# Six projections of the last two batches as seven block products each, in an RWKV block on one Trainium2 core

## The chip, the cores and the metric

The kernel runs on one NeuronCore of a Trainium2 chip. It uses TensorE for matrix products (PE in the profile, its weight loads PEld), VectorE (DVE), ScalarE (ACT) and GpSimd (POOL) for elementwise work, and SyncE (SP) to issue DMAs. TensorE writes to PSUM; GpSimd works in SBUF only. The metric is the device time of one execution in microseconds; lower is better.

## The reference

One RWKV block over 8 batches of 256 tokens with 512 channels (32 heads of 16). All in float32. Cut to what matters here:

```python
xn = _ln(x, ln1_w, ln1_b); sx = _token_shift(xn, state[:, i1])
x5 = xn[:, :, None] + sx[:, :, None] * (maa_stack + xxx)     # five mixes
r, k, v = x5[..3] @ Wr.T, x5[..0] @ Wk.T, x5[..2] @ Wv.T     # 512 x 512 each
g = silu(x5[..4] @ Wg.T)
# recurrent scan over the tokens, then a norm over each head: att
x = x + att * g @ Wo.T                                       # "o"
xn2 = _ln(x, ln2_w, ln2_b); sx2 = _token_shift(xn2, state[:, i0])
xk, xr = xn2 + sx2 * ffn_maa_k, xn2 + sx2 * ffn_maa_r
rr = sigmoid(xr @ ffn_Wr.T)                                  # "fr"
kk = square(relu(xk @ ffn_Wk.T))                             # "fk"
x = x + rr * (kk @ ffn_Wv.T)                                 # "fv"
```

So each batch has eight projections by a 512 x 512 matrix, of which the last four (o, fk, fr, fv) come after the scan.

## The kernel before

The kernel collects all its work as a list of some 2,700 operations (`Plan`), each with its engine, the buffers that it reads and writes, and a function that emits it. `Plan.ORDER` is one long list of numbers written out by hand: the operations are emitted in this order, so each engine's queue takes its operations in the order of the list, and a buffer of a pool is given to an operation when the list reaches it.

For each batch there are three stages. `inputs_of_scan` normalizes x, builds the five mixes and makes r, k, v, w and g. `scan` does the recurrence: for each of 16 slices a DMA spreads v over a `vs` tile (128 x 1024), VectorE multiplies it by k (L864; k was copied into PSUM, `kp`, by ScalarE at L845), VectorE scans along the tokens (L866, the decay lies in PSUM as `wrep`), GpSimd multiplies by r (L869, in place in an `st8` tile), and TensorE gathers four such slices (L877). `rest` norms att, multiplies by g (L941 in the last batch), and does the four projections: o with x added (L949), the second layer norm (L493 to L562), fk with relu and square (L958, L959), fr with tanh (L967; the sigmoid is (tanh + 1)/2), and fv, whose result is multiplied by (o + 1) (L990) and gets x added (L995 on GpSimd, or L985 and L993 on VectorE in the last batch) before it is written out.

A projection is 16 matmuls of 128 x 128 by 256 columns, or 8 with 512 columns. `project` (fk) puts channels on the partitions; `project_tokens` (o, fr, fv) puts tokens there, with the two 128-token halves of the activations as the weights of TensorE and rows of the matrix as the moving operand. Both go through `mul` (L330); each matmul in float32 leaves two records in the trace. Results lie in one of six PSUM buffers `ps`.

Weights of the four projections of `rest` are loaded anew for each batch into four `Ws` tiles (128 x 2 x 512, two for each matrix). Other pools that the change uses: `mix` (14 tiles of 128 x 512), `vs` and `st8` (six of 128 x 1024 each), and `k`, `r`, `v`, `w` (three of each, 128 x 512).

The order at the end is this. Projections of batch 6 and 7 are written fr6, fv6, o7, fk7, fr7, fv7. After the last scan and the last gather of batch 7 TensorE does fr6, o7, one half of fv6, the transposes of the layer norm, the other half of fv6, then fk7, fr7 and fv7. fv7's second half of tokens is cut into pieces of 256, 128 and 128 channels, each written out by itself.

Of the kernel before, what the change touches and what calls it, by code (L numbers as in the profile page):

```python
# [11 lines left out]
P = 128  # L12
# [9 lines left out]
AHEAD = (4, 5, 6, 7)  # L22
HALF = 0.5
# [37 lines left out]

class Op:


    def __init__(self, engine, us, outs, ins, emit, mode):
        self.engine, self.us, self.emit, self.mode, self.narrow, self.table = engine, us, emit, mode, False, None
        self.bufs = list(dict.fromkeys([*outs, *ins]))
        self.before, self.wire = [], 0


class Plan:
# [197 lines left out]
def tile_rwkv_block(  # L269
# [44 lines left out]
    def new(pool, name):  # L314
        return Buf(pool, name, VIEWS.get(pool, lambda t: t))
# [780 lines left out]
```

## Time and profile before

| | |
|---|---|
| median of 3 runs | 603.5 us (602.17 to 604.19) |
| the profiled execution | 603.54 us |
| its span, first to last instruction | 601.7 us |
| TensorE busy / VectorE busy / ScalarE busy / GpSimd busy | 592.1 / 537.5 / 504.9 / 507.2 us |
| granted TensorE clock | 0.996 |
| DMA | 128.07 MB, 213 GB/s |

Busy time is the time in which an engine had at least one instruction under way. In a row of the timeline stand start and duration in microseconds, engine, line, operation, output <- inputs by buffer name, shapes, and count; several equal instructions in a row are merged. A group row ends with busy time and the mean duration in nanoseconds. In the rows by stretches of time (from:to) stand the length, the busy time of PE, PEld, DVE, ACT and POOL with the number of instructions, the granted TensorE clock, the DMA share and GB/s.

### The profile page before, as it was taken

The page shows a single profiled execution, that of the slowest core. Times are in us where ns is not written, and L with a number is a line of the kernel's source. Part 1 is how long each engine was busy: PE and PEld are TensorE (multiplying, and loading weights), DVE is VectorE, ACT ScalarE, POOL GpSimd, SP SyncE. Part 2 cuts the span into 40 slices and gives each one's busy share as a digit, 9 for nine tenths or more (in the row PEclk, how much of TensorE's full clock was granted, in tenths as well). Part 3 has the DMA queues.
Part 4 walks back from the last instruction along what each step waited for, and adds up shares of the span by engine and source line. Part 5 has one row for each costly group of instructions (what it writes and reads, how often), then busy time and mean ns, then how long its engine had stood idle before and what let it go on. Part 6 is the DMA issues. An engine that isn't in the chain of part 4 may idle for free.

```text
span 601.7 us, 19771 instructions
## 1 busy us (share of the span) xinstructions
PE 592.1 (98%) x8308; PEld 343.5 (57%) x8308; DVE 537.5 (89%) x500; ACT 504.9 (84%) x1198; POOL 507.2 (84%) x390
## 2 busy tenths in 40 slices
PE   8999998999999999999999999999999999999997
PEld 7575556457536775366553754465645574455464
DVE  5799999999999999899889999999999999996342
ACT  5898779899999999989999988989987879964531
POOL 0689999899989999999979898999798999888030
PEclk9999999899999999999999999999999999999999
DMA  8797768887888869778888897687899887952533
GB/s 295 228 246 196 186 155 246 239 221 203 224 229 246 221 163 276 220 203 230 203 250 221 224 251 212 163 234 206 219 257 242 214 234 206 280 180 73 189 122 109
DMA packets 55497, 128.07 MB, mean 213 GB/s; under 512 B 6112, under 2 KB 13680, under 8 KB 55408
## 3 DMA queue, kind: packets, MB, share of 16 engines
q1 hardware_dynamic: 51040, 122.61, 74.9%
q10 hardware_dynamic: 4368, 4.20, 2.2%
q8 instruction: 65, 1.06, 0.8%
q14 instruction: 24, 0.20, 0.1%
HBM read 118.39 MB, written 8.40 MB: 211 GB/s over the span
## 4 chain that ended last, share of the span: by engine, by line
PE 83%; POOL 10%; ACT 2%; DVE 2%; issue 2%; DMA 0%; SPq 0%; POOLq 0%; ACTq 0%
PE ps L330 70%; PE ps L877 8%; POOL st L869 5%; POOL mix L701 3%; PE ps L741 2%; PE ps L525 2%; POOL vs L861 1%; DVE st L493 1%; POOL rk L814 1%; PE ps L903 1%; DMA sq<-in_x 0%; POOL mix L569 0%; PE ps L819 0%; POOL att L833 0%; POOL mix L729 0%
## 5 line engine op out<-in xcount | busy, mean ns | idle before, releaser
L866 DVE TENSOR_TENSOR_SCAN st<-wrep,vs 128x1024 f32<-128x1024 f32 x128 | 288.2, 2277 | 2.2 <-POOL mix L701 0.6
L869 POOL TENSOR_TENSOR st<-st,r 128x1024 f32<-128x1024 f32 x128 | 254.7, 2002 | 8.3 <-DVE st L866 5.1
L864 DVE TENSOR_TENSOR vs<-vs,ps 128x1024 f32<-128x1024 f32 x125 | 147.7, 1208 | 6.1 <-ACT vs L857 4.1
L330 PE MATMUL ps<-Ws,mix 128*32 128x512 f32 (+3 forms) x836 | 115.5, 585 | 0.0
L330 PEld LDWEIGHTS ps<-Ws,mix 128*32 128x32 f32 (+1 forms) x836 | 39.0, 118 | 61.9 <-issue 54.6
L701 POOL TENSOR_TENSOR mix<-mix,xn 128x512 f32<-128x512 f32 x62 | 67.1, 1095 | 7.1 <-DVE mix L695 4.1
L330 PE MATMUL ps<-mix,Wv 128*32 128x256 f32 (+1 forms) x880 | 62.2, 389 | 2.1 <-POOL mix L701 2.1
L877 PE MATMUL ps<-st,con 128*32 128x256 f32 x1024 | 61.9, 380 | 0.0
L330 PE MATMUL ps<-mix,Wr 128*32 128x256 f32 (+1 forms) x760 | 60.7, 380 | 0.2 <-ACT v L772 0.2
L330 PE MATMUL ps<-mix,Wg 128*32 128x256 f32 (+1 forms) x904 | 60.4, 379 | 0.0
L330 PE MATMUL ps<-mix,Wk 128*32 128x256 f32 (+1 forms) x856 | 59.5, 380 | 0.0
L330 PE MATMUL ps<-mix,Ws 128*32 128x256 f32 (+1 forms) x928 | 57.5, 379 | 0.0
L330 PE MATMUL ps<-Ws,g 128*32 128x512 f32 (+1 forms) x464 | 56.9, 592 | 0.5 <-POOL g L943 0.5
L569 POOL TENSOR_TENSOR mix<-mix,xn 128x512 f32<-128x512 f32 x44 | 47.5, 1091 | 7.3 <-ACT mix L567 7.3
L330 PEld LDWEIGHTS ps<-mix,Wv 128*32 128x32 f32 (+1 forms) x880 | 39.8, 117 | 22.0 <-issue 4.4
L330 PEld LDWEIGHTS ps<-mix,Wr 128*32 128x32 f32 (+1 forms) x760 | 39.5, 119 | 17.2 <-issue 1.1
L827 ACT COPY att<-ps 32x256 f32<-32x256 f32 x128 | 46.5, 364 | 2.7 <-PE ps L819 0.5
L330 PEld LDWEIGHTS ps<-mix,Wg 128*32 128x32 f32 (+1 forms) x904 | 37.2, 114 | 18.9 <-issue 1.0
L330 PEld LDWEIGHTS ps<-mix,Wk 128*32 128x32 f32 (+1 forms) x856 | 38.5, 115 | 16.6 <-issue 1.2
L877 PEld LDWEIGHTS ps<-st,con 128*32 128x32 f32 x1024 | 34.4, 110 | 23.6 <-issue 2.8
L330 PEld LDWEIGHTS ps<-mix,Ws 128*32 128x32 f32 (+1 forms) x928 | 35.9, 113 | 20.3 <-issue 1.2
L689 ACT ACTIVATE ps<-ps,vec 128x256 f32<-128x256 f32 x112 | 44.3, 449 | 3.5 <-PE ps L330 3.1
(134 smaller groups left out, 940.0 us busy)
## 6 DMA issues: line engine op xcount, KB each, us to landing
vs<-vo SPq DMA_DIRECT2D x128, 512.0 KB, 5.9
Ws<-in_fk SPq DMA_DIRECT2D x16, 512.0 KB, 6.2
Ws<-in_fr SPq DMA_DIRECT2D x16, 512.0 KB, 5.2
Ws<-in_wo SPq DMA_DIRECT2D x16, 512.0 KB, 5.9
Ws<-in_fv SPq DMA_DIRECT2D x16, 512.0 KB, 4.9
x<-in_x SPq DMA_DIRECT2D x11, 512.0 KB, 6.3
vo<-v ACTq DMA_DIRECT2D x15, 256.0 KB, 3.7
out<-o SPq DMA_DIRECT2D x15, 256.0 KB, 5.3
```

The source lines that it names most:

```text
L330: nc.tensor.matmul(out[i : i + n], lhsT=w[:, i : i + n], rhs=x, start=first, stop=final)
L493: dve(512, [st], [s], lambda st=st, s=s: nc.vector.bn_stats(out=st(), in_=s()))
L525: nc.tensor.transpose(ps()[:, m, n * P : (n + 1) * P], xh[n]()[:, k * P : (k + 1) * P], idt())
L569: gp(512, t, [t, xn[q]], lambda q=q, t=t: nc.gpsimd.tensor_tensor(t(), t(), xn[q]()[:, :, 1 : T + 1], ALU.add))
L689: act(256, p_, [p_, vec], lambda g=g, q=q, m=m, p_=p_: nc.scalar.activation(p_()[:, m, :], p_()[:, m, :], AF.Identity, bias=col(f"maa_{g}" ...
L701: gp(512, t, [t, xn[q]], lambda q=q, t=t: nc.gpsimd.tensor_tensor(t(), t(), xn[q]()[:, :, 1 : T + 1], ALU.add))
L741: nc.tensor.matmul(pd()[i : i + 32, 0, :], lhsT=w, rhs=src[k // 2]()[:, k % 2, :], start=(k == begin), stop=(k == end))
L827: act(350, atts[q], [pc], lambda i=32 * (2 * q + m), m=m, q=q, h=32 * h: nc.scalar.copy(atts[q]()[h : h + 32, m, :], pc()[i : i + 32, 0, :]))
L864: dve(4 * T, [vs], [vs, kp], lambda m=m, vs=vs, kp=kp: nc.vector.tensor_tensor(vs(), vs(), kp()[:, m : m + 1, :].to_broadcast([P, 4, T]), ...
L866: dve(4 * T, [st], [w, vs], lambda w=w, vs=vs, st=st: nc.vector.tensor_tensor_scan(st().rearrange("p n t -> p (n t)"), w().rearrange("p n ...
L869: gp(4 * T, st, [st, r], lambda m=m, st=st, r=r: nc.gpsimd.tensor_tensor(st(), st(), r()[:, m : m + 1, :].to_broadcast([P, 4, T]), ALU.mul ...
L877: nc.tensor.matmul(pat()[32 * i : 32 * i + 32, 0, :], lhsT=con()[:, s : s + 32], rhs=done[i]()[:, j, :], start=(j == 0), stop=(j == 3),)
```

## The change

Six projections, o7, fk7, fr7, fv7, fr6 and fv6, are done by Strassen's algorithm in Winograd's form. The activations and the matrix are each cut into 2 x 2 blocks; eight block products become seven, and sums of blocks are added around them: four sums of activation blocks (named x0 to x3 below, each 128 x 256 elements), four sums of weight blocks (w0 to w3, 128 x 512), and seven sums of products (128 x 256) for the result. Two lines say which pool holds the weight sums and which engine makes them, and which weights are streamed into `vs` tiles in place of `Ws`:

```diff
+SEVEN = {"o7": ("vs", "DVE"), "fk7": ("st8", "POOL"), "fr7": ("st8", "POOL"), "fv7": ("st8", "POOL"), "fr6": ("krvw", "DVE"), "fv6": ("krvw", "POOL")}
+STREAMS = {"fr7": "vs", "fv7": "vs"}
```

Activation sums are made on VectorE. The core of the new functions:

```diff
+    def tensor(engine, n, out, a, b, how):
+        if engine == "DVE":
+            dve(n, [out], [a, b], lambda: nc.vector.tensor_tensor(out(), a(), b(), how))
+        else:
+            gp(n, out, [a, b], lambda: nc.gpsimd.tensor_tensor(out(), a(), b(), how))
+
+    def seven(name, w, src, tokens=True):
...
+        for out, x, y, how in ((0, a[1, 0], a[1, 1], ALU.add), (1, s[0], a[0, 0], ALU.subtract),
+                               (2, a[0, 0], a[1, 0], ALU.subtract), (3, a[0, 1], s[1], ALU.subtract)):
+            tensor(es, ns, s[out], x, y, how)
+        for out, x, y, how in ((0, b[0, 1], b[0, 0], ALU.subtract), (1, b[1, 1], t[0], ALU.subtract),
+                               (2, b[1, 1], b[0, 1], ALU.subtract), (3, t[1], b[1, 0], ALU.subtract)):
+            tensor(et, nt, t[out], x, y, how)
+        pairs = {1: (a[0, 0], b[0, 0]), 2: (a[0, 1], b[1, 0]), 3: (s[3], b[1, 1]), 4: (a[1, 1], t[3]),
+                 5: (s[0], t[0]), 6: (s[1], t[1]), 7: (s[2], t[2])}
...
+                            mul(out()[:, cols], l()[:, k, :], r()[:, k, cols], k == 0, k == 1)
...
+        one = product(1)
+        act(256, old, [one], lambda: nc.scalar.copy(old(), one()))
+        tensor("DVE", T, spare[0], product(6), old, ALU.add)
+        tensor("DVE", T, spare[1], product(5), spare[0], ALU.add)
+        return product, old, *spare
+
+    def into(blocks, product, old, six, five):
...
+        tensor("DVE", T, blocks[1, 0], six, product(4), ALU.subtract)
+        tensor("DVE", T, blocks[0, 1], five, product(3), ALU.add)
+        last = product(7)
+        tensor("DVE", T, blocks[1, 0], blocks[1, 0], last, ALU.add)
+        tensor("DVE", T, blocks[1, 1], five, last, ALU.add)
+        if (0, 0) in blocks:
+            tensor("DVE", T, blocks[0, 0], old, product(2), ALU.add)
+
+    def added(blocks, product, old, six, five):
...
+        for i, t in (((1, 0), six), ((0, 1), five), ((1, 1), five), ((0, 0), old)):
+            tensor("DVE", T, blocks[i], blocks[i], t, ALU.add)
```

A product is read from PSUM by the sums that use it; `old`, `six` and `five` lie in SBUF, in `mix` tiles. o7 adds its sums straight onto x (`added`); the others write them to kk, o or a spare tile (`into`). relu, square and tanh of these projections, and the closing (o + 1) * y and + x, go by blocks of 256. In the last batch fv7's second product is cut in two halves of 128 channels, and its blocks are written out as each is done.

The list of numbers is new as a whole, from its first line on; the list has 2,811 operations now. At the end it puts the work like this:

- TensorE, from the last gather: fr6's products 1 and 2, the head norm of batch 7, half of g7's first projection (it stood before the last gather), fr6's 6, 3, 5; o7's 1, 2, 5, 6, 3, 4, 7; fv6's 7 and 1, fr6's 4, fv6's 6 and 2, transposes, fv6's 4, transposes, fr6's 7, fv6's 5 and 3; fk7's 2, 3, 1, 5, 6, 4, 7; then fr7 and fv7 mixed, with fr7's 7, fv7's 7, fr7's 3, a half of fv7's 2 and fv7's 3 at the end.
- VectorE, from the last scan: fr6's w0, w1, one (o+1)*y of batch 5, fv6's x2, fr6's w3, w2, the two last att adds, the other (o+1)*y; x0 of fv6, x0 of fr6, x1 of fv6, x1 of fr6, x3 of fv6; o7's w0, fr6's x3, o7's w2, w1; att by its norm twice; o7's w3, the first g product, fr6's x2, the second g product, o7's x0; then the sums of o7 between its x1, x2, x3 and some of fr6.
- GpSimd, from the last scan: the last product by r, xr6 twice, + x of batch 5 twice, weight sums fr7.w0, fv7.w0, fr7.w1, fv7.w1, fv6.w0, w2, w1, w3, fr7.w2, w3, fk7.w0, w2, w1, w3, then sx, fv7.w3, xr7 twice, + x of batch 6 four times, fv7.w2.
- The weight loads of fr6, o7, fr7 and fv7 are issued around the last scan; the second half of fv6's weights follows fr6's third product, fk7's follow o7's.

More of the change, by code (lines that the diff above doesn't have):

```diff
@@ L59, in __call__, with __init__ @@
         return self.view(self.buf())
+class Half(Part):
+    def __init__(self, buf, view):
+        super().__init__(buf, view)
+        self.writers, self.readers, self.before = [*buf.writers], [], set()
+class Group:
+    def __init__(self, parts, view):
+        self.parts, self.view = parts, view
+    def __call__(self):
+        return self.view()
 class Op:
@@ L66, in __init__ @@
         self.engine, self.us, self.emit, self.mode, self.narrow, self.table = engine, us, emit, mode, False, None
-        self.bufs = list(dict.fromkeys([*outs, *ins]))
+        self.bufs = list(dict.fromkeys(getattr(b, "buf", b) for b in [*outs, *ins]))
         self.before, self.wire = [], 0
@@ L206, in add @@
     def add(self, engine, us, outs, ins, emit, mode=None, kb=0, part=False):
-        outs, ins = ([getattr(b, "buf", b) for b in bs] for bs in (outs, ins))
+        outs, ins = ([p if hasattr(p, "writers") else p.buf for b in bs for p in getattr(b, "parts", [b])] for bs in (outs, ins))
         op = Op(engine, us, outs, ins, emit, mode)
@@ L427, in stream @@
     def stream(name, src, b):
-        tiles = [new("Ws", f"W{name}{b}_{h}") for h in range(2)]
+        pool = STREAMS.get(f"{name}{b}", "Ws")
+        tiles = [new(pool, f"W{name}{b}_{h}") for h in range(2)]
+        if pool != "Ws":
+            for t in tiles:
+                t.view = lambda t: t.rearrange("p j t -> p (j t)").rearrange("p (k e) -> p k e", k=2)
         load_pairs(tiles, src)
@@ L597, in project_tokens, with halves @@
         return ps
+    def halves(pool, name, n, width):
+        each = {"mix": 2 * T, "st8": 4 * T, "vs": 4 * T}[pool] // (2 * width)
+        tiles = [new(pool, f"{name}{i}") for i in range(-(-n // each))]
+        return [Half(tiles[i // each], lambda t, j=i % each * 2 * width: t.rearrange("p m t -> p (m t)")[:, j : j + 2 * width]
+                     .rearrange("p (k w) -> p k w", k=2)) for i in range(n)]
+    def tensor(engine, n, out, a, b, how):
[3 more added lines that the diff above has]
+            gp(n, out, [a, b], lambda: nc.gpsimd.tensor_tensor(out(), a(), b(), how))
@@ new lines, in seven, with product, mm @@
+    def seven(name, w, src, tokens=True):
+        pool, engine = SEVEN[name]
+        tile_of = lambda k: k.buf
+        W2, X2 = [tile_of(w[0]), tile_of(w[2])], src
+        wide = {(h, c): Part(W2[h], lambda t, c=c: t[:, :, c * T : (c + 1) * T]) for h in range(2) for c in range(2)}
+        slim = {(h, n): x if isinstance(x, Half) else Part(x, lambda t, n=n: t[:, :, n * P : (n + 1) * P])
+                for h in range(2) for n in range(2) for x in [X2[h][n] if isinstance(X2[h], list) else X2[h]]}
+        ws = (halves(pool, f"tw{name}_", 4, T) if pool != "krvw" else [
+            Part(new(p, f"tw{name}_{p}"), lambda t, lo=int(p == "v"): t[:, :, lo : lo + T]) for p in pool])
+        xs = halves("mix", f"tx{name}_", 4, P)
+        old, *spare = halves("mix", f"old{name}_", 6 if name[:2] == "fv" else 3, P)
+        if tokens:
+            old, *spare = (Half(h.buf, lambda t, h=h: h.view(t).rearrange("p k w -> p (k w)")) for h in (old, *spare))
+        if tokens:
+            a = {i: slim[i[1], i[0]] for i in ((0, 0), (0, 1), (1, 0), (1, 1))}
+            b, s, t, es, et, ns, nt = wide, xs, ws, "DVE", engine, T, 2 * T
+        else:
+            a = {(c, h): wide[h, c] for h in range(2) for c in range(2)}
+            b, s, t, es, et, ns, nt = slim, ws, xs, engine, "DVE", 2 * T, T
+        for out, x, y, how in ((0, a[1, 0], a[1, 1], ALU.add), (1, s[0], a[0, 0], ALU.subtract),
[6 more added lines that the diff above has]
+                 5: (s[0], t[0]), 6: (s[1], t[1]), 7: (s[2], t[2])}
+        def product(i, cols=slice(0, T)):
+            l, r = pairs[i]
+            buf = new("ps", f"pw{name}_{i}")
+            out = Part(buf, lambda t: t[:, 0, :] if tokens else t[:, :, 0:P])
+            def mm():
+                for m in range(1 if tokens else 2):
+                    for k in range(2):
+                        if tokens:
+                            mul(out()[:, cols], l()[:, k, :], r()[:, k, cols], k == 0, k == 1)
+                        else:
+                            mul(out()[:, m, :], l()[:, k, m * P : (m + 1) * P], r()[:, k, :], k == 0, k == 1)
+            pe((0.86 if tokens else 0.89) * (cols.stop - cols.start) / T, [buf], [l, r], mm)
+            return out
+        one = product(1)
[3 more added lines that the diff above has]
+        return product, old, *spare
@@ new lines, in into @@
+    def into(blocks, product, old, six, five):
[9 more added lines that the diff above has]
+            tensor("DVE", T, blocks[i], blocks[i], t, ALU.add)
+        tensor("DVE", T, blocks[1, 0], blocks[1, 0], product(4), ALU.subtract)
+        tensor("DVE", T, blocks[0, 1], blocks[0, 1], product(3), ALU.add)
+        last = product(7)
+        for n in range(2):
+            tensor("DVE", T, blocks[1, n], blocks[1, n], last, ALU.add)
+        tensor("DVE", T, blocks[0, 0], blocks[0, 0], product(2), ALU.add)
@@ L946, in rest @@
         x2 = load_x(b, "x2")
-        for n in range(NT):
-            t, ps = x2[n], project_tokens(Wo, ys, n, f"pso{b}_{n}")
-            dve(512, [t], [ps, t], lambda t=t, ps=ps: nc.vector.tensor_tensor(
-                t(), ps().rearrange("p m t -> p (m t)"), t(), ALU.add))
+        blocks = {(n, c): Half(x2[n].buf, lambda t, n=n, c=c: t[:, n, c * T : (c + 1) * T]) for n in range(NT) for c in range(2)}
+        if f"o{b}" in SEVEN:
+            added(blocks, *seven(f"o{b}", Wo, ys))
+            x2 = [Group([blocks[n, c] for c in range(2)], t) for n, t in enumerate(x2)]
+        else:
+            for n in range(NT):
+                t, ps = x2[n], project_tokens(Wo, ys, n, f"pso{b}_{n}")
+                dve(512, [t], [ps, t], lambda t=t, ps=ps: nc.vector.tensor_tensor(
+                    t(), ps().rearrange("p m t -> p (m t)"), t(), ALU.add))
+            blocks = {(n, c): Part(x2[n].buf, h.view) for (n, c), h in blocks.items()}
         xn, sx = normed(x2, 2, 0, b, last)
@@ L954, in rest @@
         kk = []
-        for q in range(NQ):
+        if f"fk{b}" in SEVEN:
+            ts = [new("mix", f"kk{b}_{q}") for q in range(NQ)]
+            kk = [[Half(t, lambda t, n=n: t[:, :, n * P : (n + 1) * P]) for n in range(NT)] for t in ts]
+            parts = {(q, n): kk[q][n] for q in range(NQ) for n in range(NT)}
+            into(parts, *seven(f"fk{b}", Wfk, xk, False))
+            for t in parts.values():
+                act(256, t, [t], lambda t=t: nc.scalar.activation(t(), t(), AF.Relu, scale=HALF**0.5))
+                act(256, t, [t], lambda t=t: nc.scalar.activation(t(), t(), AF.Square))
+        for q in range(NQ if not kk else 0):
             t = new("mix", f"kk{b}_{q}")
@@ L962, in rest @@
         Wfr = stream("fr", fr, b)
-        os = []
-        for n in range(NT):
+        os, outs = [], {}
+        if f"fr{b}" in SEVEN:
+            os = [new("o", f"o{b}_{n}") for n in range(NT)]
+            outs = {(n, c): Half(os[n], lambda t, c=c: t[:, c * T : (c + 1) * T]) for n in range(NT) for c in range(2)}
+            into(outs, *seven(f"fr{b}", Wfr, xr))
+            for t in outs.values():
+                act(256, t, [t], lambda t=t: nc.scalar.activation(t(), t(), AF.Tanh, scale=HALF), "tanh")
+        for n in range(NT if not os else 0):
             o = new("o", f"o{b}_{n}")
@@ L970, in rest @@
         Wfv = stream("fv", fv, b)
+        if f"fv{b}" in SEVEN:
+            product, old, six, five, *spare = seven(f"fv{b}", Wfv, kk)
+            sums = dict(zip(((0, 1), (1, 0), (1, 1)), spare))
+            if last:
+                into(sums, product, old, six, five)
+                y, x_ = outs[0, 0], blocks[0, 0]
+                dve(T, [old], [y, old], lambda: nc.vector.scalar_tensor_tensor(old(), y(), 1.0, old(), ALU.add, ALU.mult))
+                tensor("DVE", T, x_, x_, old, ALU.add)
+                two = [product(2, slice(h * P, (h + 1) * P)) for h in range(2)]
+            else:
+                sums[0, 0] = old
+                into(sums, product, old, six, five)
+            for i, t in sums.items():
+                o, t2 = outs[i], blocks[i]
+                dve(T, [o], [o, t], lambda o=o, t=t: nc.vector.scalar_tensor_tensor(o(), o(), 1.0, t(), ALU.add, ALU.mult))
+                tensor("DVE" if last else "POOL", T, o, o, t2, ALU.add)
+                if last:
+                    n, cols = i[0], slice(i[1] * T, (i[1] + 1) * T)
+                    dma(None, lambda o=o: o(), lambda n=n, cols=cols: out[b, n * P : (n + 1) * P, cols], 131, o)
+            if last:
+                for h, t in enumerate(two):
+                    o = Half(outs[0, 0].buf, lambda t, h=h: t[:, h * P : (h + 1) * P])
+                    o.writers = [*outs[0, 0].writers]
+                    o.readers = [*outs[0, 0].readers]
+                    t, x_ = Part(t.buf, lambda t, h=h: t[:, 0, h * P : (h + 1) * P]), Group([blocks[0, 0]], lambda h=h: blocks[0, 0]()[:, h * P : (h + 1) * P])
+                    dve(P, [o], [o, t], lambda o=o, t=t: nc.vector.scalar_tensor_tensor(o(), o(), 1.0, t(), ALU.add, ALU.mult))
+                    tensor("DVE", P, o, o, x_, ALU.add)
+                    dma(None, lambda o=o: o(), lambda h=h: out[b, 0:P, h * P : (h + 1) * P], 66, o)
+            else:
+                for n in range(NT):
+                    dma(None, os[n], lambda n=n: out[b, n * P : (n + 1) * P, :], 256, Group([outs[n, c] for c in range(2)], os[n]))
+            return
         for n in range(NT):
```

238 rows, old and new, of the table ORDER are left out of this document.

## The prediction

> **What bounds the kernel now.** I read the page first, then the table by stretches of time, then the chain of waits and the timeline of the last 60 us.
>
> ```profile
> span 601.7 us, 19771 instructions
> PE 592.1 (98%) x8308; PEld 343.5 (57%) x8308; DVE 537.5 (89%) x500; ACT 504.9 (84%) x1198; POOL 507.2 (84%) x390
> ...
> PE 83%; POOL 10%; ACT 2%; DVE 2%; issue 2%; DMA 0%; SPq 0%; POOLq 0%; ACTq 0%
> ...
> core 0: us, PE busy (x) PEld busy (x) DVE busy (x) ACT busy (x) POOL busy (x), PEclk, DMA share, GB/s
> ...
> 500.00:520.00 20.00, 20.00 (x308) 9.75 (x300) 20.00 (x13) 19.14 (x40) 20.00 (x14) 1.00 0.83 217
> 520.00:540.00 20.00, 20.00 (x188) 9.12 (x184) 19.85 (x22) 14.34 (x38) 15.83 (x13) 1.00 0.76 230
> 540.00:550.00 10.00, 10.00 (x192) 6.06 (x188) 9.97 (x8) 6.27 (x13) 9.98 (x8) 1.00 0.02 5
> ...
> 549.00:602.00 53.00, 49.09 (x269) 27.10 (x260) 16.56 (x33) 18.75 (x33) 11.10 (x10) 0.99 0.43 139
> ```
>
> TensorE is the chain's engine for 83% of the span. Until 550 us VectorE (DVE) is full as well; from 549 on it works 16.6 of 53 us and GpSimd (POOL) 11.1, while TensorE works 49. So there is a tail where only TensorE counts, and the change puts its sums there.
>
> ```profile
> 544.79 4.46 DVE L866 TENSOR_TENSOR_SCAN st<-wrep,vs 128x1024 f32<-128x1024 f32 x2
> ...
> 547.73 3.95 POOL L869 TENSOR_TENSOR st<-st,r 128x1024 f32<-128x1024 f32 x2
> ...
> 552.06 1.91 PE L877 MATMUL ps<-st,con 128*32 128x256 f32 x32
> ...
> 562.37 7.03 PE L330 MATMUL ps<-Ws,g 128*128 128x512 f32 x16
> ...
> 577.56 7.09 PE L330 MATMUL ps<-mix,Ws 128*128 128x256 f32 x32
> ...
> 558.90 10.51 PE ps L330 x24
> 569.43 0.69 DVE x L949
> 570.12 1.19 DVE st L493 x2
> ...
> 573.19 1.09 PE ps L525 x8
> 574.28 24.19 PE ps L330 x88
> 598.50 0.30 DVE sq L983
> ```
>
> The last scan ends at 544.79 + 4.46 = 549.25; I count "+t" from there. The o7 projection runs from +13.1. Behind it stands batch 7's layer norm, covered by fv6; then fk7, fr7 and fv7 without a gap. The last result adds end at 599.1, and the out transfer takes the 2.6 us to 601.7. The profiled execution took 603.54, so 1.84 us lie around its span; the median of the runs is 603.5, and the sums hold for both.
>
> **What the change removes: 5.0 us of TensorE.** A projection in tokens form is 16 records of 512 columns: 562.37 to 569.23 is 6.86 us, 0.43 each. The fk7 form takes 32 records of 256 columns, 577.56 to 584.49, 0.217 each. One block product has 4 records of 256 columns, 0.87 us; seven are 6.06. For fk7 a product is 8 records of 128 columns, as in the transposes (8 in 1.09 us with start and end, so 0.11 to 0.14 each); I take 0.87 again, and 0.25 more per product at the upper end. Six projections save 6 x 0.84 = 5.0 us. All six stand behind the last gather and in front of the end, where TensorE ends last, so this is saved whole if the blocks arrive in time.
>
> **What it adds at the end: 0.7 us.** The last product, fv7's third, is followed by three dependent VectorE instructions of 256 (sum, (o+1)*y, plus x), at 0.42 to 0.46 each 1.3 us, where today a pair of 128 takes 0.6. With every sum hidden: 603.5 - 5.0 + 0.7 = 599.2.
>
> ScalarE gains six copies of a first product and about ten halves in place of wholes, some 6 us beside 18.75 of 53 in the tail; that stays hidden. The weight loads are as many as before; those of fr7 and fv7 start earlier, in scan buffers. One load matters: the second half of fv6's weights waits for fr6's third product, and behind it on GpSimd's queue stand nine weight sums.
>
> **What the sums cost.**
>
> ```profile
> 18.77 1.28 DVE L698 TENSOR_TENSOR mix<-mix,xn 128x512 f32<-128x512 f32 x2
> ...
> 418.34 1.08 DVE L724 TENSOR_TENSOR mix<-ps,sx 128x256 f32<-128x256 f32 x3
> ...
> L698 DVE TENSOR_TENSOR mix<-mix,xn 128x512 f32<-128x512 f32 x2 | 1.3, 682 | 0.0
> ...
> L724 DVE TENSOR_TENSOR mix<-ps,sx 128x256 f32<-128x256 f32 x28 | 10.8, 413 | 1.6 <-ACT ps L722 1.6
> ...
> 540.66 2.14 POOL L569 TENSOR_TENSOR mix<-mix,xn 128x512 f32<-128x512 f32 x2
> ...
> Ws<-in_fv SPq DMA_DIRECT2D x16, 512.0 KB, 4.9
> ```
>
> Independent VectorE sums of 512 follow each other at 1.28 - 0.68 = 0.60 us, of 256 at (1.08 - 0.41)/2 = 0.335; dependent ones need 0.42 and more. GpSimd needs 1.05 for 512. From the last scan on, VectorE gets 81 instructions of 256, 8 weight sums of 512 and some 10 us of others (what stands there today, less the adds that go): at the fast rates 27.1 + 4.8 + 10.4 = 42 us, at the slow ones 51. GpSimd gets 16 weight sums (16.8 us) and 11.6 of others. Against a tail of 47 us both fit, VectorE narrowly.
>
> Now the place that decides. Nearly every VectorE instruction of today has one input in PSUM: the multiply L864 (kp), the scan (wrep). The new sums of x and weights have both in SBUF, and so has everything on GpSimd. Only one place shows the two together:
>
> ```profile
> L864 DVE TENSOR_TENSOR vs<-vs,ps 128x1024 f32<-128x1024 f32 x125 | 147.7, 1208 | 6.1 <-ACT vs L857 4.1
> L869 POOL TENSOR_TENSOR st<-st,r 128x1024 f32<-128x1024 f32 x128 | 254.7, 2002 | 8.3 <-DVE st L866 5.1
> ...
> 12.96 0.69 DVE L550 TENSOR_TENSOR sx<-xn 128x512 f32<-128x512 f32 x1
> ...
> 575.08 1.04 POOL L550 TENSOR_TENSOR sx<-xn 128x512 f32<-128x512 f32 x1 [20.24 <-ACT xn L546]
> ...
> 575.42 1.24 DVE L550 TENSOR_TENSOR sx<-xn 128x512 f32<-128x512 f32 x1
> ```
>
> With PSUM inputs, 125 multiplies run beside GpSimd at an even 1.21. With two SBUF inputs, the same subtraction took 0.69 with GpSimd idle (12.96) and 1.24 when GpSimd had begun 0.34 us earlier. It ended at 576.66, 0.54 us after GpSimd's end at 576.12: as if it had stood still until then. The Trainium skill, "SBUF — State Buffer", section "SBUF: two separate sides", states this rule: a VectorE instruction with two SBUF inputs and a GpSimd one that reads SBUF hold a shared port exclusively, and the later one fully blocks. By that rule the trace agrees (0.54 after the other's end), and the change would lose more than it gains; without it the sum stays 599.2.
>
> I price it from this row alone. A VectorE sum that meets GpSimd waits up to the rest of its instruction (1.05, or 1.96 for a scan product); I let the two alternate. At the lower bound a sum waits for nothing. At the upper one, all 28 us of GpSimd's tail stand in VectorE's way.
>
> *First stretch, last scan to o7's first product.* In the new order VectorE does fr6's and o7's weight sums and the x sums of fr6 and fv6 there, GpSimd the last scan products, xr6, o5, and the weight sums of fr7, fv7, fv6. Waits: fr6.w0 0.5 and w1 2.0 (scan products), fv6.x2 0.4, fr6.w3 1.05; then fr6.x0, fv6.x1, fr6.x1, fv6.x3, o7.w0, fr6.x3, o7.w2 at 1.05 each, 7.35. Together 11.3 us; then GpSimd stands before fv6's load and the rest passes freely. VectorE's own work up to the first g is 9 x 0.60 + 4 x 0.60 + 9 x 0.335 = 10.8, and 1.1 of waiting for the gather, so o7 starts at +11.9 without the port (TensorE's own earlier work ends there too). With it the gather's 1.1 vanishes in the waits: +22. **Loss 10.**
>
> *Second stretch, o7's seven products.* Its x sums and the adds of six and five onto x27 (both in SBUF) meet fv6.w2, w1, w3 and fr7.w2, w3: x2 0.7, x3 1.05, two adds 1.0 each, and what lies beside products taken off: **loss 3.5.** The layer norm waits for the last of them.
>
> *Third stretch.* sx, xk and fk7's x sums meet GpSimd's sx, fv7.w3 and xr7, and (o+1)*y meets fv6's + x: two to four waits, of which products hide some. I take **1**, between 0 and 4.
>
> Forecast: 599.2 + 10 + 3.5 + 1 = 613.7, say **613.5**.
>
> ```profile
> 104.00:116.00 12.00, 11.32 (x182) 6.21 (x185) 11.93 (x8) 10.27 (x21) 10.74 (x8) 0.86 0.91 246
> ```
>
> TensorE then has gaps of some microseconds. In the one stretch with such gaps around it the granted clock was 0.86 over 12 us, 1.7 us lost; I count that in the upper end only, once or twice. In front of the tail the order is new too, though of the same instructions; today TensorE has no gap from 118.6 on, and I allow 1 us either way for it.
>
> **The rivals.** *All sums hidden, faster.* The mechanism is TensorE alone: the tail is as long as its products. For it speaks that the new order keeps TensorE fed to the end when I walk it with the fast rates (o7's first product waits 0.2 us), with all seven products of fv6 and two of fr6 laid under the layer norm. Against it speaks the row at 575.42. It decides if the waits sum to under 603.5 - 599.2 = 4.3 us, that is under 0.2 us for each of the 24 sums that stand beside GpSimd in the first two stretches. 599.2, give or take 2.
>
> *VectorE's rate becomes the bound, no port.* Most added sums hang on a sum just before or on a product, so they run at 0.42 instead of 0.335. Then VectorE needs 51 us from the last scan: 549.25 + 51.4 + 2.6 + 1.84 = 605.1. For it speaks that the L724 group's mean is 0.41; against it, that the order interleaves independent sums. Range 603 to 607.
>
> *The port, but milder*, when GpSimd itself waits for weights at the start (seven half-MB loads lie within some 15 us there, and one takes 4.9) and so leaves VectorE room: 605 to 608.
>
> **How the numbers follow.** The port as walked, 608 to 620: 0.60, predicted 613.5 (599.2 + 17.5 + two clock losses at the top). Milder: 0.06. VectorE's rate: 0.13. All hidden: 0.21. The range should reach into the last: 599.5 to 620 holds the first three and over a third of it. About 0.3% (1.8 us) is what a measurement of this kernel can tell from no change. Faster than that is most of "all hidden", 0.20; no change is the lower part of "VectorE's rate", 0.07; slower is the rest, 0.73.
>
> **What would show each step.** TensorE's busy time in the tail 5 us less, products at 0.87: the saving. VectorE sums of x or weights with durations of 0.9 to 1.6 instead of 0.42 and 0.69, ending just after a GpSimd instruction, while sums with a PSUM input stay at 0.41: the port. GpSimd's weight sums longer than 1.09: the same from the other side. TensorE idle for several microseconds before o7's first and third products: the first two stretches. I would be wrong if those sums keep 0.42 and 0.69 beside a busy GpSimd, or if the last scan ends much earlier than 549 less 1.7 (half a g7 projection is moved behind it), which would give the tail more room.

## The result and the profile after

The changed kernel takes 618.79 us (median of 4 runs, 616.26 to 619.96) against 603.2 us for the kernel before in the same comparison: a ratio of 1.0253, 95% interval 1.0215 to 1.029. It is 15.6 us slower, and 5.3 us above the predicted 613.5.

From the profile page of the changed kernel, the span, the busy times and the shares of the chain that ended last; then its table by stretches of 10 us (length, PE, PEld, DVE, ACT, POOL, granted clock, DMA share, GB/s):

```profile
span 617.9 us, 19984 instructions
PE 594.0 (96%) x8344; PEld 347.1 (56%) x8344; DVE 584.3 (95%) x581; ACT 511.8 (83%) x1214; POOL 532.4 (86%) x408
...
PE 80%; DVE 11%; ACT 3%; issue 3%; DMA 1%; SPq 0%; POOL 0%; DVEq 0%
...
550.00:560.00 10.00, 8.32 (x108) 4.19 (x100) 10.00 (x13) 4.95 (x7) 7.51 (x7) 1.00 0.56 190
560.00:570.00 10.00, 3.96 (x9) 3.20 (x10) 9.58 (x13) 2.08 (x4) 4.24 (x3) 0.71 0.22 77
570.00:580.00 10.00, 6.72 (x23) 4.98 (x22) 7.96 (x12) 2.07 (x3) 6.65 (x5) 0.84 0.27 93
580.00:590.00 10.00, 9.47 (x45) 7.90 (x44) 8.05 (x18) 1.97 (x7) 5.32 (x4) 0.94 0.16 54
```

The place is easy to see. TensorE does more records than before (8344 against 8308), but smaller ones; it is busy 1.9 us more in a span 16.2 us longer, and VectorE's share of the last chain has gone from 2% to 11%. Between 550 and 570 us VectorE is busy nearly all the time, and TensorE only 12.3 of 20 us. The granted clock is 0.71 from 560 to 570 us and comes back over the next 20 us (0.84, then 0.94), so part of the work that TensorE does have is done slowly.

VectorE's and GpSimd's timelines of that place (start, duration; equal instructions in a row are merged):

```profile
540.20 6.64 DVE L985 TENSOR_TENSOR_SCAN st<-wrep,vs 128x1024 f32<-128x1024 f32 x3
546.76 0.66 DVE L638 TENSOR_TENSOR k<-Ws 128x512 f32<-128x512 f32 x1
547.46 2.38 DVE L638 TENSOR_TENSOR r<-Ws,k 128x512 f32<-128x512 f32 x1
...
550.99 1.58 DVE L638 TENSOR_TENSOR w<-r,Ws 128x512 f32<-128x512 f32 x1
...
554.35 5.69 DVE L638 TENSOR_TENSOR mix<-mix,mix 128x256 f32<-128x256 f32 x5
```

```profile
546.92 2.36 POOL L988 TENSOR_TENSOR st<-st,r 128x1024 f32<-128x1024 f32 x1 [0.18 <-DVE st L985]
549.25 2.77 POOL L599 TENSOR_TENSOR mix<-mix,xn 128x512 f32<-128x512 f32 x2
554.51 2.44 POOL L1166 TENSOR_TENSOR o<-o,x 128x512 f32<-128x512 f32 x2 [2.49 <-DVE o L1161]
556.91 2.86 POOL L640 TENSOR_TENSOR st<-vs 128x512 f32<-128x512 f32 x2
559.73 3.11 POOL L640 TENSOR_TENSOR st<-vs,st 128x512 f32<-128x512 f32 x2
...
571.82 1.26 POOL L640 TENSOR_TENSOR v<-Ws,Ws 128x512 f32<-128x512 f32 x1 [7.58 <-DMA Ws<-in_fv]
```

Two pairs tell what happens. VectorE's second weight sum (547.46) ends at 549.84, 0.56 us after GpSimd's scan product (ends 549.28). Its third one (550.99) ends at 552.57, 0.55 us after GpSimd's pair (ends 552.02). That is the 0.54 us of the single row at 575.42 on which the prediction priced the port (its word for the path to SBUF that the two engines share): the VectorE sum ends as if it had stood still until GpSimd was through, and had then done its work. Five activation sums of 256 columns in a row (554.35) take 5.69 us, 1.14 each, while GpSimd has the two + x of batch 5 at 1.22 and two weight sums at 1.43; the weight sums behind them take 1.56 instead of the 1.05 assumed. Then GpSimd waits 7.58 us for the second half of fv6's weights.

The groups of instructions from the last scan on show that it is the instructions that read SBUF alone and not VectorE as a whole; the column ahead of the last is the mean in nanoseconds:

```profile
L638 DVE TENSOR_TENSOR mix<-mix,mix 128x256 f32<-128x256 f32 x15 | 12.1, 829 | 0.1
L638 DVE TENSOR_TENSOR mix<-mix,ps 128x256 f32<-128x256 f32 x14 | 5.5, 411 | 0.1
...
L592 DVE SCALAR_TENSOR_TENSOR mix<-sx,vec,xn 128x256 f32<-128x256 f32 x4 | 4.6, 1180 | 0.0
```

The same operation on the same shape takes 829 ns on the mean with both inputs in SBUF and 411 ns with one of them in PSUM (`ps`).

Last, TensorE's timeline with the marks by which all runs below are compared:

```profile
566.04 2.08 PE L356 MATMUL ps<-Ws,mix 128*128 128x256 f32 x4 [6.22 <-DVE att L1045]
567.91 1.91 PE L356 MATMUL ps<-k,mix 128*128 128x256 f32 x4
569.62 2.57 PE L356 MATMUL ps<-Ws,g 128*128 128x256 f32 x8
...
574.73 1.13 PE L356 MATMUL ps<-vs,mix 128*128 128x256 f32 x4 [1.68 <-DVE mix L638]
577.46 1.78 PE L356 MATMUL ps<-Ws,mix 128*128 128x256 f32 x4 [1.60 <-DVE mix L638]
...
591.44 0.49 PE L356 MATMUL ps<-mix,Ws 128*128 128x128 f32 x2
```

The last scan ends at 540.20 + 6.64 = 546.84, o7's first product starts at 569.62, fk7's first at 591.44, the span ends at 617.9. TensorE stood idle for 6.22 us before 566.04: fr6's product 3 had to wait for the PSUM buffer that `att` by its norm (L1045, VectorE) was to free, and that instruction stood behind the blocked sums in VectorE's queue.

### The profile page after: what moved, and what is told of

Read it like the earlier page. It is cut to its first block, busy times and chain, and to the rows that moved or that the text cites. A ratio compares the mean times of both kernels' runs of the same rounds, so it can differ in the third digit from the quotient of the medians.

```text
span 617.9 us, 19984 instructions
## 1 busy us (share of the span) xinstructions
PE 594.0 (96%) x8344; PEld 347.1 (56%) x8344; DVE 584.3 (95%) x581; ACT 511.8 (83%) x1214; POOL 532.4 (86%) x408
## 4 chain that ended last, share of the span: by engine, by line
PE 80%; DVE 11%; ACT 3%; issue 3%; DMA 1%; SPq 0%; POOL 0%; DVEq 0%
PE ps L356 67%; PE ps L996 8%; DVE mix L638 3%; DVE st L985 2%; PE ps L860 2%; PE ps L555 1%; DMA Ws<-in_wv 1%; DVE mix L592 1%; DVE vs L638 1%; DVE vs L983 1%; ACT rk L1051 1%; ACT sq L1051 1%; PE ps L1022 0%; PE ps L938 0%; SPq L345 0%
## 5 line engine op out<-in xcount | busy, mean ns | idle before, releaser
L356 PE MATMUL ps<-Ws,mix 128*32 128x512 f32 (+3 forms) x772 | 95.4, 582 | 8.1 <-DVE att L1045 6.2
L356 PEld LDWEIGHTS ps<-Ws,mix 128*32 128x32 f32 (+1 forms) x772 | 30.3, 114 | 60.7 <-issue 42.9
L996 PE MATMUL ps<-st,con 128*32 128x256 f32 x1024 | 63.2, 387 | 0.9 <-DVE mix L843 0.9
L356 PE MATMUL ps<-mix,Wv 128*32 128x256 f32 (+1 forms) x928 | 60.1, 380 | 0.0
L356 PE MATMUL ps<-mix,Ws 128*32 128x256 f32 (+2 forms) x824 | 54.0, 376 | 1.3 <-DVE mix L592 1.3
L356 PE MATMUL ps<-Ws,g 128*32 128x512 f32 (+1 forms) x456 | 52.6, 591 | 0.0
L356 PEld LDWEIGHTS ps<-mix,Wr 128*32 128x32 f32 (+1 forms) x832 | 37.5, 116 | 18.7 <-issue 1.6
L356 PEld LDWEIGHTS ps<-mix,Wv 128*32 128x32 f32 (+1 forms) x928 | 36.5, 113 | 19.8 <-issue 1.3
```

The costliest lines, as they stand in the source:

```text
L356: nc.tensor.matmul(out[i : i + n], lhsT=w[:, i : i + n], rhs=x, start=first, stop=final)
L996: nc.tensor.matmul(pat()[32 * i : 32 * i + 32, 0, :], lhsT=con()[:, s : s + 32], rhs=done[i]()[:, j, :], start=(j == 0), stop=(j == 3),)
```

## The experiments

### Two engines by themselves

The first question was whether the port is a fact of this chip or a reading of one row. A kernel that leaves out the whole block runs groups of equal instructions (mostly eight) on VectorE, on GpSimd, and on both:

```python
for i in range(8):   # one of the groups; the others change the inputs
    nc.gpsimd.tensor_tensor(gs[i % 4][:], ga[:, 0:512], gb[:, 0:512], ALU.subtract)
    nc.vector.tensor_tensor(ds[i % 4][:, 0:256], xa[:, 0:256], xb[:, 0:256], ALU.subtract)
```

> A small kernel by itself, not the block: stretches of equal instructions on VectorE and GpSimd, alone and together; it leaves the reference's computation out. Port theory: 256-wide VectorE sums with both inputs in SBUF take 0.42 us alone and 1.0 to 1.4 us while GpSimd runs 512-wide sums, and GpSimd's go from 1.05 to 1.3 to 1.5 us; the 512-wide ones go from 0.69 to 1.3 to 1.8; with one input in PSUM they stay at 0.41 and GpSimd at 1.05. Rate theory (the tail is long only because of the number of VectorE instructions): 0.42 and 0.69 in every stretch. Open: a tensor_scalar with one SBUF input beside GpSimd, which took 0.54 in the profile of before and 1.03 in the one of after.

Its groups by line; on VectorE first L48 alone, L55 beside GpSimd, L64 beside GpSimd with one input in PSUM, L75 a one-input `tensor_scalar` alone and L68 the same beside GpSimd:

```profile
L48 DVE TENSOR_TENSOR ds<-xa,xb 128x256 f32<-128x256 f32 x8 | 2.8, 419 | 0.0
...
L55 DVE TENSOR_TENSOR ds<-xa,xb 128x256 f32<-128x256 f32 x8 | 9.2, 1213 | 0.0
...
L64 DVE TENSOR_TENSOR ds<-xa,wide 128x256 f32<-128x256 f32 x16 | 5.4, 411 | 0.0
...
L75 DVE TENSOR_SCALAR ds<-xa,xb 128x512 f32<-128x512 f32 x8 | 3.7, 538 | 0.0
...
L68 DVE TENSOR_SCALAR ds<-xa,xb 128x512 f32<-128x512 f32 x8 | 9.4, 1246 | 0.0
```

```profile
L51 POOL TENSOR_TENSOR gs<-ga,gb 128x512 f32<-128x512 f32 x8 | 9.8, 1260 | 0.0
...
L54 POOL TENSOR_TENSOR gs<-ga,gb 128x512 f32<-128x512 f32 x8 | 11.1, 1415 | 0.0
...
L62 POOL TENSOR_TENSOR gs<-ga,gb 128x512 f32<-128x512 f32 x8 | 9.8, 1261 | 0.0
```

A sum of 256 goes from 419 to 1213 ns when GpSimd works beside it (L54 is its partner) and stays at 411 with an input in PSUM (partner L62, itself undisturbed at 1261). So the blocking is real, for a sum it goes when one input comes from PSUM, and both sides pay. GpSimd's sum by itself took 1260 ns, not the 1.05 us that the prediction and this run's expectation took from the kernel before. The `tensor_scalar`, which has one tensor input (its two scalars per partition lie in SBUF as well), is blocked too, 538 to 1246 ns; the prediction had counted sums only. Not everything that reads SBUF alone is: in run e1 below the layer norm's statistics (BATCH_NORM_STATS2, one SBUF input) took 0.68 and 0.69 us at 570.00 and 571.04, in the middle of GpSimd's weight sums, as they did in e5 with GpSimd idle (0.69). The Trainium skill, "SBUF — State Buffer", section "SBUF: two separate sides", names VectorE instructions in a two-port mode beside those with two SBUF inputs as holders of the same lock. The 1246 ns agree with that as far as the blocking goes; which mode the instruction ran in is not in the trace.

### The sums of one engine made harmless

Two runs take the collision away from either side, and a third from both, with all instructions left in their places. The sums changed in this way no longer give the block's values.

```diff
 # e1: VectorE's 32 block sums take their second input from a PSUM tile; the same for et, nt and t
-            tensor(es, ns, s[out], x, y, how)
+            (from_psum if es == "DVE" else lambda *a: tensor(es, *a))(ns, s[out], x, y, how)
 # e2: GpSimd's 16 weight sums cover 2 of 256 columns
+            if n == 2 * T:
+                gp(n, out, [a, b], lambda: nc.gpsimd.tensor_tensor(out()[:, :, 0:2], a()[:, :, 0:2], b()[:, :, 0:2], how))
+                return
```

> The changed kernel, in which the 32 block sums that VectorE makes ahead of the products read their second input from a PSUM tile (the scan's decay) in place of the right block; so these sums have other values, and the count, sizes, order and waits of all instructions are kept. Port theory: these sums fall to 0.41 and 0.69 us; the excess that they show in the profile of after (about 10 us up to o7's first product, 2.7 in o7, 1.5 later) and the clock lost in the gaps go: 602 to 606 us. Rate theory and load theory (waits for weight loads and PSUM buffers in the new order): 616 to 620 us as before.

> The changed kernel, in which GpSimd's 16 weight sums cover 2 of 256 columns of each block; the rest of those sums is left out. VectorE's instructions, all loads, the order and the waits stay. Port theory: VectorE's waits behind those 16 instructions go, those behind the scan products, xr6, o5, sx and xr7 stay (about 5 us of the first stretch, 1 to 2 of the last): 604 to 609 us. Rate theory and load theory: 616 to 620 us.

> The changed kernel with both cuts at once: VectorE's 32 block sums read their second input from PSUM, and GpSimd's 16 weight sums cover 2 of 256 columns (the rest of those sums is left out). Order, loads, products and counts stay. If the port is the whole loss, the sum of the prediction with every sum hidden comes out: 598 to 601 us. If VectorE's rate or the waits for loads and PSUM buffers set a second bound: 602 to 605 us.

e1: 605.44 us, ratio 1.0048 (1.0027 to 1.007). e2: 602.99 us, 1.0 (0.9986 to 1.0014). Both together (e5): 597.99 us, 0.9907 (0.9882 to 0.9933). e1 lies in the range expected of the port, e5 on its lower edge, and e2 is 1 us better than its range. e1 and e2 are far from the 616 to 620 us expected if VectorE's rate or the loads had been the cause, and e5 stays under the 602 to 605 of a second bound behind the port. The groups of e1, VectorE from the last scan on:

```profile
L639 DVE TENSOR_TENSOR mix<-g,wrep 128x256 f32<-128x256 f32 x3 | 1.1, 407 | 0.0
...
L643 DVE TENSOR_TENSOR x<-x,mix 128x256 f32<-128x256 f32 x5 | 5.2, 1081 | 0.0
```

The sums that now read PSUM (`wrep`) have gone back to 407 ns. The adds onto x that were left alone still meet GpSimd, now at 1081 ns: the collision has moved on to them. In e2 it is the other way round, and the fifteen sums of the group shown above fall from 829 to 543 ns, not to 411: GpSimd's + x of batches 5 and 6 are still in their way (five of the sums, beside the + x of batch 5, take 3.55 us):

```profile
L638 DVE TENSOR_TENSOR mix<-mix,mix 128x256 f32<-128x256 f32 x15 | 7.8, 543 | 0.1
```

With both sides harmless, the table by stretches of e5 has TensorE full from the last scan to its last product, at full clock:

```profile
550.00:560.00 10.00, 10.00 (x109) 6.77 (x99) 9.45 (x21) 7.40 (x12) 3.06 (x8) 1.00 0.89 283
560.00:570.00 10.00, 10.00 (x51) 8.75 (x50) 9.48 (x27) 2.65 (x7) 1.58 (x9) 1.00 0.36 116
570.00:580.00 10.00, 9.94 (x74) 9.24 (x72) 9.89 (x24) 5.94 (x12) 5.21 (x6) 1.00 0.01 2
```

So the whole loss, and the gain that the seven products would bring, hang on VectorE and GpSimd meeting. The two are not additive: e1 takes 13.4 us off and e2 15.8, but both together 20.8, since a pair of colliding instructions has one member on either side.

### The clock

Behind the 6.22 us in which TensorE stood idle, two products took 1.87 and 1.71 us from start to start (566.04, 567.91, 569.62) instead of the 0.86 that a product takes in e5, at a granted clock of 0.71. Six matmuls of 512 columns into a PSUM tile that nobody reads any more fill part of the gap:

```diff
+    def warm():
+        for _ in range(6):
+            nc.tensor.matmul(wide()[:, 0:2, :].rearrange("p j t -> p (j t)"), lhsT=idt(), rhs=w2a(), start=True, stop=True)
+
+    pe(5.2, [wide], [idt, w2a], warm)
```

> The changed kernel with 6 extra matmuls (12 records of 512 columns, 5.2 us at full clock) into the scan's free PSUM tile in TensorE's gap ahead of fr6's third product; nothing else is changed. If the low granted clock behind the gap (0.71 and 0.84 in the two slices of 10 us after it) is part of the chain: 615 to 617 us, 2 to 3 below the changed kernel, and a granted clock of 1 from 566 on. If VectorE alone sets the pace there: the same 618 to 619.

615.55 us, ratio 1.022 (1.0199 to 1.0242). Its table by stretches:

```profile
560.00:570.00 10.00, 8.80 (x27) 5.00 (x28) 10.00 (x12) 2.42 (x6) 5.68 (x4) 1.00 0.33 104
570.00:580.00 10.00, 8.48 (x38) 6.64 (x37) 9.93 (x21) 2.07 (x3) 7.63 (x6) 1.00 0.48 155
580.00:590.00 10.00, 8.06 (x31) 6.07 (x31) 9.10 (x18) 3.15 (x10) 5.68 (x6) 0.83 0.01 2
```

The clock is 1.00 where it was 0.71 and 0.84, and the median is 3.2 us lower. The two intervals overlap (this one's upper end 1.0242, the changed kernel's lower end 1.0215), so the gain of about 3 us is likely but not shown clear of the noise. The trace shows it in the first place: the same two products now take 0.96 and 0.89 us, and o7 starts 1.7 us sooner after the scan (table below). A later gap, at the layer norm, then costs clock in its turn (0.83 in 580 to 590). The Trainium skill, "TensorE: Matmul & The Clock Gate", section "Part 1: The HAM clock gate", has an idle window halve the clock; a mean of 0.71 over 10 us fits with part of the stretch at half speed, as do the two products at twice their time.

### Other orders

If the collision is the cause, an order that keeps the sums apart should help. I searched orders with a model in which GpSimd's instructions and VectorE's with all inputs in SBUF take turns, and ran four. v6 re-orders the last 520 operations of the changed kernel, v0 the same for the computation of before, v3 has seven products in fk7, fr7 and fv7 alone. v7 leaves everything up to the last scan as it is in the changed kernel and re-orders the operations behind it. The diff is the list of numbers, and for v3 and v0 the two lines of the change (and two lines of bookkeeping that emit nothing):

```diff
 # v3
+SEVEN = {"fk7": ("st8", "POOL"), "fr7": ("st8", "POOL"), "fv7": ("st8", "POOL")}
+STREAMS = {"fk7": "vs", "fr7": "vs", "fv7": "vs"}
 # v0
+SEVEN = {}
+STREAMS = {}
```

> The changed kernel with another order of its last 520 operations, nothing else: looked for by moving single operations, with a model of my own in which GpSimd and a VectorE instruction with all operands in SBUF hold the port one at a time (GpSimd's weight sums at 1.22 us). Port theory: the loss belongs to the order as much as to the sums; the model puts it 13 us below the changed kernel and 3 below the kernel before: 599 to 606 us. Rival (so many sums crowd the port in any order): 609 to 618 us.

> No projection in seven products: the computation of the kernel before, with the order of its last 520 operations looked for in the same way. The model puts it 3.3 us below the kernel before: 599 to 601 us. If the order of before was already as good as the chip allows: 602 to 605 us. It is the yardstick for the two other orders.

> Three projections in seven products (fk7, fr7, fv7), all weight sums on GpSimd in the time in which it is idle after the scan, the three weight matrices loaded into scan buffers, the last 520 operations ordered in the same way. Saving by the terms of the prediction: 3 x 0.84 - 0.7 = 1.8 us against the kernel of the same kind of order without it; the model puts it 1.2 below that one and 4.4 below the kernel before: 598 to 601 us. Rival (the sums behind the layer norm stand in the chain): 603 to 607 us.

> The same six projections and the same front as the changed kernel; only the operations behind the last scan stand in another order, searched with a model in which GpSimd instructions and VectorE instructions with all inputs in SBUF take turns (GpSimd's weight sums at 1.22 us). Theory (it is the taking of turns, so where the sums stand matters): last scan again at about 546.8, and by the model 12.5 us less between it and the end than in the changed kernel: 606 us, 603 to 611. Rival (the sums cost about the same wherever they stand behind the scan, since TensorE waits for them there in any order): 616 to 619, as the changed kernel. If the last scan ends more than 1 us later than at 546.8, the front was disturbed and the run only tells about the stretch behind it.

All four missed the model's times; v6 came out in the range of its rival, by which the sums crowd the port in any order, and v7 between its two. v6: 615.28 us, 1.019 (1.0164 to 1.0217). v0: 605.37 us, 1.004 (1.002 to 1.0059). v3: 607.35 us, 1.0058 (1.0036 to 1.0081). v7: 613.49 us, 1.0155 (1.0092 to 1.0217). Two stretches of v6 show why the totals of the first three tell little about the collision:

```profile
500.00:520.00 20.00, 18.30 (x277) 8.63 (x272) 16.71 (x12) 18.83 (x40) 14.40 (x11) 1.00 0.86 235
520.00:540.00 20.00, 17.70 (x136) 7.01 (x128) 18.55 (x22) 15.73 (x40) 18.03 (x13) 0.91 0.65 176
```

TensorE lost 1.7 and 2.3 us there, ahead of all block sums but one, and the last scan ended at 551.07, 4.2 us later than in the changed kernel. From there to the end of the span, however, v6 took 61.3 us (612.4 - 551.07) where the changed kernel took 71.1 (617.9 - 546.84), with all six projections in seven products: the order behind the scan does matter, and the front ate part of it. The model did not know the waits of that part well enough, and even the computation of before got 0.4% slower by the search. v7 was made after that, to keep the front out of it; its last scan ends at 546.60, and its tail takes 66.9 us. Its timeline on TensorE:

```profile
558.14 1.13 PE L353 MATMUL ps<-Ws,g 128*128 128x256 f32 x4
561.30 1.13 PE L353 MATMUL ps<-Ws,g 128*128 128x256 f32 x4 [2.03 <-DVE g L1057]
...
573.59 1.11 PE L552 MATMUL ps<-idt,xh 128*128 128x128 f32 x4 [4.24 <-DVE xh L526]
```

and on GpSimd:

```profile
566.56 1.56 POOL L637 TENSOR_TENSOR k<-Ws 128x512 f32<-128x512 f32 x1 [9.95 <-DMA Ws<-in_fv]
```

Here o7's first product starts 11.5 us after the scan and its second 14.7, instead of 22.8 for the first in the changed kernel, so the order does decide the first stretch. Part of that is only moved: one product stands ahead of o7 in this order, five in the changed kernel, and four products are 3.5 us. And now TensorE has nothing to do under the layer norm (4.24 us idle ahead of 573.59; the granted clock is 0.83 in 560 to 570 and 0.66 in 570 to 580): all eight products of fr6 and fv6 that need weight sums stand behind it in this order, and GpSimd, which makes fv6's sums, had waited 9.95 us for its weights. Of the 11.2 us won in front, 5.3 are left at the end. No version with the full computation was faster than the kernel before. Whether some order could be stays open: v6's tail has v7's beaten by 5.6 us, but no run joins such a tail to the front of the changed kernel.

## Why the prediction was right, and where its sizes were off

Four marks divide the tail: the last scan's end, o7's first product, fk7's first product, the end of the span. e5 does the same instructions with nothing in the way and gives each stretch's length without the collision. Each row of the table is one execution, 0.3 to 1.9 us above the median of its runs, so differences of some tenths between rows mean little. The two marks that no row above shows are these; of e5:

```profile
539.24 6.64 DVE L993 TENSOR_TENSOR_SCAN st<-wrep,vs 128x1024 f32<-128x1024 f32 x3
...
557.85 2.12 PE L356 MATMUL ps<-Ws,g 128*128 128x256 f32 x8
...
572.77 1.29 PE L356 MATMUL ps<-mix,Ws 128*128 128x128 f32 x8
...
580.45 1.89 PE L356 MATMUL ps<-st,mix 128*128 128x256 f32 x8
582.17 1.03 PE L356 MATMUL ps<-vs,mix 128*128 128x256 f32 x4
```

| us | last scan ends | to o7's first product | to fk7's first product | to the end | span |
|---|---|---|---|---|---|
| e5, both sides harmless | 545.88 | 11.97 | 14.92 | 23.7 | 596.5 |
| e2, GpSimd's weight sums harmless | 546.49 | 16.97 | 15.15 | 24.5 | 603.1 |
| e1, VectorE's sums harmless | 547.58 | 12.10 | 20.52 | 25.1 | 605.3 |
| e3, matmuls in the gap | 548.28 | 21.06 | 21.37 | 24.8 | 615.5 |
| the changed kernel | 546.84 | 22.78 | 21.82 | 26.5 | 617.9 |

The end of the span, first in the changed kernel, then before:

```profile
610.95 2.34 PE L356 MATMUL ps<-vs,mix 128*128 128x256 f32 x12
...
614.35 0.62 DVE L638 TENSOR_TENSOR o<-o,x 128x128 f32<-128x128 f32 x2
```

```profile
596.73 1.73 PE L330 MATMUL ps<-Ws,mix 128*128 128x128 f32 x14
...
598.82 0.29 DVE L985 TENSOR_TENSOR sq<-sq,x 128x128 f32<-128x128 f32 x1
```

**All sums hidden, 599.2.** That was the sum without the port, and e5 took 598.0. Within that, two small terms were off. A block product takes 0.86 us from start to start (580.45 to 582.17 for two in e5) and 0.895 in fk7's form, where 0.87 was taken for both: a saving of 4.8 us instead of 5.0. At the end the last adds finish 1.7 us after TensorE instead of 0.65, and the out transfer lands 2.9 us after them instead of 2.6: 1.4 more in place of 0.7. The last scan was 3.4 us earlier in e5 than before, of which the half g7 projection moved behind it is about 1.7; the rest is what the new front gave, a little over the 1 us allowed either way.

**The first stretch, loss 10.** Measured 22.78 - 11.97 = 10.8, and the two ends themselves were forecast at 22 and 11.9. The sum is nearer than its parts. The walk had 3.95 us of waits on GpSimd's scan products and xr6 and seven of 1.05, two of them on + x of batch 5 and five on weight sums, less 1.1 of waiting that they cover: 4.95 without the weight sums and 5.25 for these. With the weight sums harmless (e2) 5.0 are left, so they cost 5.8. But part of both is the low clock, which the walk did not have here: the two products ahead of o7 took 3.58 us from start to start (566.04 to 569.62), and 3.11 in e2, instead of 1.73. So the clock is 1.85 of the 10.8 and the port about 9.0, a little under the walk; that the total came out so close is in part luck. That all of it hangs on the collision, the gap and its clock too, is shown by e1, which leaves 0.1.

**The second stretch, loss 3.5.** Measured 21.82 - 14.92 = 6.9. This is the term that was mis-sized. The waits themselves were right in sum: VectorE's four blocked instructions there (an add onto x, x1, x2 and x3, from 571.87, 573.28, 574.93 and 575.93 on) took 1.49, 1.39, 1.07 and 1.48 us instead of 0.42, together 3.75 too much, as much as the walk's 0.7 + 1.05 + 1.0 + 1.0; and TensorE was idle for 3.8 us (1.68, 1.60 and 0.53 in its timeline). The other 3.1 us is time in which TensorE was busy: 18.0 us in place of e5's 14.9 for the same 73 records, at a mean granted clock of 0.89. Two products from 569.62 and three from 577.46 took 2.40 and 4.38 us from start to start, where the same ones took 1.95 and 2.59 in e5, so about 2.2 us of it is the clock and the rest, by all appearance, the starts and ends around the gaps. The clock was counted in the upper end of the range alone, although the walk itself had put TensorE gaps into the forecast. With the 1.85 us of the first stretch it cost about 4.1 us, a little more than the two losses of 1.7 by which the range was stretched to 620. e3 does not have this stretch much shorter (21.37), since other gaps open in it: there as in e1 (20.52, at full clock) TensorE waits for adds onto x and for the layer norm's `tensor_scalar` xh. Those two took 1081 and 1602 ns on the mean in e1, where e5 has 419 and 543; in the changed kernel xh took 1028. I had not counted xh, which has one tensor input.

**The third stretch, loss 1.** Measured 26.5 - 23.7 = 2.7, within the 0 to 4 given. xk (L592) stands at its beginning, at 1180 ns where e5 has 837, and fk7's products wait for it, 0.92 and 0.41 us; another 1.08 us is a wait for VectorE ahead of 606.11.

**ScalarE hidden.** It was: 2.0 to 5.0 of every 10 us behind 550. **VectorE's rate as the bound (605.1)** fell: e5 keeps VectorE at 9.4 to 9.9 of 10 us and loses nothing on TensorE. The sum behind that rival was off as well: at the slow rates that the prediction names, 81 x 0.42 + 8 x 0.69 + 10.4 is 49.9 us and not 51.4, which makes it 603.6. **The milder port (605 to 608)**, by GpSimd waiting for weights, did happen as a wait, 7.6 us for fv6's weights before 571.82, but only after the first stretch's harm was done, as the walk had it. **The last scan** was to be up to 1.7 earlier; it was 2.4 earlier.

Put together, in spans: 596.5 + 1.0 (the later scan) + 10.8 + 6.9 + 2.7 = 617.9. The prediction's 14.5 us of port became 20.4: about 16.3 of port and 4.1 of clock. A base 1.2 lower took a little of that back. So the measured 618.79 lies near the top of the range of 599.5 to 620, where the prediction had put the clock losses that its forecast left out.

## What to carry to other kernels

An engine with idle time in the profile is not free if the work put on it shares a path with another engine's work: look for a row in which the two run together before counting the idle time as cover. Here a VectorE sum with one input in PSUM stood beside GpSimd at no cost (411 ns, and GpSimd's 1261 against 1260 alone), while one with both inputs in SBUF took 1213 instead of 419. So where a sum can take an operand straight from PSUM, that decides more than the count of instructions. When a chain of such sums feeds TensorE, add the price of its lower clock after a gap (about 4.1 us here) to the forecast itself and not only to the range.

## What the runs showed of the hardware that was not expected

GpSimd's sum of 512 columns took 1.26 us by itself in the isolated run and 1.29 in a quiet place of e1 (570.18 and 571.44), where the rows of before had 1.04 and 1.07 for the same shape on other operands. What makes the difference was not tried.

The taking of turns is not quite whole. Beside VectorE's sums of 256 in the isolated run, seven of GpSimd's eight instructions took 1.44 us and the last, by itself, 1.26, and a pair came every 1.40 us (24.11, 25.52, 26.92 and so on). By themselves GpSimd's instructions follow each other at 1.22 us and VectorE's at 0.34, so strict turns would have made 1.56.
